# Two transformer layers: batch 1 prepared beside the first maxima, and a rearranged end of layer 0

## The chip, the cores and the metric

The kernel runs on one core of a Trainium2 chip. The metric is device time in microseconds (us). The times of the kernel before are three runs: 2031.5, 2032.39 and 2035.87, median 2032.39. Engines are PE (matrix products), DVE (vector), ACT (scalar functions), POOL (general purpose), and SP, which here only issues transfers.

## The reference

The input x is 8 batches of 1024 rows of 128 numbers. Two layers follow each other, each of an attention part and a feed-forward part, each part behind a layer normalisation and with its result added to x:

```python
x = x + _L0_attn_ref(_layernorm(x), Wq, Wkv_down, Wk_up, Wv_up, Wo)   # softmax attention, 8 heads of 32
x = x + _L0_ffn_ref(_layernorm(x), gate_w, w1, b1, w2, b2)            # 2 of 14 experts per row, gelu, 256 wide
x = x + _L1_attn_ref(_layernorm(x), Wq, Wk, Wv, Wo)                   # cumulative linear attention, 16 heads of 8
x = x + _L1_ffn_ref(_layernorm(x), router_w, W1, b1, W2, b2)          # 1 of 8 experts with a capacity, relu, 512 wide
```

In layer 0 keys and values come from a common latent of 64 numbers per row; softmax runs over all 1024 keys. The expert layer takes the softmax of 14 logits per row, the two largest, and adds the two experts' outputs weighted by their shares, plus the row it was given, cut to plus or minus 100.

## The kernel before, in words

**Attention of layer 0.** The two weights of the low-rank path are multiplied once (`combined_weights`), so that keys and values are one projection each of the normalised rows. The work is cut into 32 blocks: a group of 4 heads of one batch (`n = 2*batch + group`) by 512 queries (`qb`). A block has 16 steps, a key chunk of 128 and a pair of heads each, so there are 512 steps, in one loop whose order is written out by hand for PE, DVE and ACT (POOL runs in the order that a scheduler gives it, save for the instructions that are `pinned`).

Each step has two kinds of score products. `largest` (line 340) computes scores with queries on partitions, and DVE takes each row's maximum (line 344). `spread` and `spread_rows` turn these into three bf16 rows per head, by way of small SP transfers. `scores` (lines 379 and 380) computes them again with keys on partitions, the maximum subtracted by a product, and ACT takes the exponential (line 383). POOL adds the exponentials of two key chunks (line 208 in the profile's rows, a helper), and `weigh` (line 397) makes the numerators and, of the added pairs, the denominators. `settle` and `divide` make the quotient.

The maxima run `LEAD = 24` steps ahead of the scores. These 24 steps form the lead, a loop of its own before the main loop: it runs maxima and, after every even step from 4 on, one piece of the list `beside`: the last projection of heads group 0, the four `values` of batch 0, four projections of group 1. A piece is a product or two on PE into one of the three banks of the PSUM pool `big` and an evacuation by ACT. The maxima of the lead alternate between `big` and `sc`, the scores' pool of three.

Everything else of the attention is hung on the main loop as pieces per step, in the table `todo`. `prepare(b)` hangs batch b on the 64 steps of the batch before: statistics on DVE, the power of -0.5 on POOL, scaling on ACT, transposes on PE with a copy by ACT, four projections of group `2*b` (steps 20 to 25), four pairs of values (32 to 37), and the projections of group `2*b + 1` 64 steps later. So batch 1 is prepared in blocks 0 to 2 and, for its second group, in block 4. `complete(b)` hangs the output projection, the second normalisation and the choice of experts.

**The end of the attention.** After the last block its half batch (512 rows) goes through the same chain with nothing beside it: normalised, turned (`turned`, lines 295 to 300), logits (471), the two largest, `count`, `rank`, `places`. `count` (539 to 557) writes the marks of the two chosen experts into a table `both` whose column 0 holds the counts so far; `rank` makes each row's place within its expert. `places` (573 to 597) makes from rank and expert the index `at` and then eight moves, indirect transfers by POOL (588), each of which stores 128 rows into the table `rows_in`, sorted by expert.

**The tables of experts.** `expert_tables` (116 to 159) counts the tiles of 256 rows that each expert needs (`grid`, `tiles`, `upto`), and makes for each tile its first row in `rows_in` (`row_j`) and its expert (`exp_j`). These two are computed on one partition with shape 1 x 77 x 14, 1078 numbers per instruction.

**The tiles of layer 0.** `tiles0` runs 72 tiles. `fetch` loads a tile by SP at a row number read from `row_j` (four tiles ahead); `stage` copies the expert's weights out of the big table by DVE (886); `turn` transposes; `hidden0` multiplies and takes gelu on ACT (901, 904); `output0` multiplies again, adds bias and input rows on DVE, and stores into `rows_out` by POOL (921). PE, DVE, ACT and SP have a written order here. At tile 8 the constants of layer 1 are made. `warm` issues one unread gather by POOL. A branch (985) follows, taken only if more than 72 tiles are needed; it isn't taken with these inputs.

**Layer 1** begins with gathers from `rows_out` by POOL (1078), two per 128 rows, waits for all rows stored, and then runs its attention and its own expert tiles, for which `expert_tables` is called a second time.

Of the kernel before, what the change touches and what calls it, by code (L numbers as in the profile page):

```python
# [8 lines left out]
F32 = mybir.dt.float32  # L9
# [69 lines left out]
def tile_two_layers(  # L79
# [12 lines left out]
    for b in range(NB):  # L92
        xb = keep.tile([P, CPB, D], F32, name=f"x{b}", tag=f"x{b}")
        xs.append(xb)
    nc.sync.dma_start(out=xs[0], in_=x[0].rearrange("(c p) d -> p c d", p=P))
    cst = keep.tile([P, C_END], F32, name="cst")
# [19 lines left out]
    def expert_tables(tab, psum, ptag, counts, ne, nt):  # L116

        tot = psum.tile([P, ne], F32, name="tot", tag=ptag)  # L120
        nc.tensor.matmul(tot, lhsT=ones, rhs=counts, start=True, stop=True)
        per = CAP0 // TW0
        grid = tab.tile([P, ne, per], F32, name="grid")
        nc.vector.tensor_tensor(
            grid, tot.unsqueeze(2).to_broadcast([P, ne, per]),
            cst[:, C_TW:C_TW + per].unsqueeze(1).to_broadcast([P, ne, per]), ALU.is_gt,
        )
        tiles = tab.tile([P, ne], F32, name="tiles")
        nc.vector.tensor_reduce(tiles, grid, AX.X, ALU.add)
        upto = tab.tile([P, ne], F32, name="upto")  # L130
        nc.vector.tensor_tensor_scan(upto, ones[:, :ne], tiles, 0.0, ALU.mult, ALU.add)
        jshape = [1, nt, ne]
# [12 lines left out]
        nc.vector.tensor_tensor(hop, lead[:, 1:], lead[:, :ne], ALU.subtract)  # L145
        hops = tab.tile(jshape, F32, name="hops")
# [3 lines left out]
        nc.vector.scalar_tensor_tensor(rj, cst[0:1, C_J:C_J + nt], float(TW0), rj, ALU.mult, ALU.add)  # L150
        nc.vector.tensor_scalar(rj, rj, lead[0:1, 0:1], float(ne * REG0), ALU.add, ALU.min)
        row_j = tab.tile([1, nt], mybir.dt.int32, name="row_j")
        nc.vector.tensor_copy(row_j, rj)
        ej = tab.tile([1, nt], F32, name="ej")
        nc.vector.tensor_reduce(ej, past, AX.X, ALU.add)
        nc.vector.tensor_scalar(ej, ej, float(ne - 1), None, ALU.min)
        exp_j = tab.tile([1, nt], mybir.dt.int32, name="exp_j")
        nc.vector.tensor_copy(exp_j, ej)
        return SimpleNamespace(exp_j=exp_j, row_j=row_j, base=base, tot=tot, upto=upto)
# [30 lines left out]
    nc.gpsimd.memset(counts, 0.0)  # L190
    found = routes.tile([P, NB, 2, CPB], U32, name="found")
    layer0w = ctx.enter_context(ExitStack())
    blob = layer0w.enter_context(tc.tile_pool(name="blob", bufs=1)).tile([P, E0, B_END], F32, name="blob")

    with ExitStack() as ph:
# [30 lines left out]
        def load_rest():  # L226
            for b in range(1, NB):
                pinned(nc.sync.dma_start, out=xs[b], in_=x[b].rearrange("(c p) d -> p c d", p=P))
# [205 lines left out]
        class Finish:  # L434
# [96 lines left out]
            def weights(self):  # L531
# [4 lines left out]
                for k, p in enumerate((self.p1, self.p2)):  # L536
                    nc.vector.tensor_tensor(shares[:, k, self.b, self.c0:self.c0 + self.n], p, s, ALU.mult)

            def count(self):

                n = self.n
                both, ahead = (
                    stat0.tile([P, E0, CPB + 1], F32, name=name, bufs=1) for name in ("both", "ahead")
                )
                if n < CPB:
                    nc.vector.memset(both, 0.0)
                nc.vector.tensor_copy(both[:, :, 0], counts)
# [25 lines left out]
            def places(self):  # L573
# [13 lines left out]
                def move(j, k):  # L587
# [6 lines left out]
                    tc.add_to_no_dep_group("rows_in", ins.ins)  # L594
                    tc.keep_in_program_order(ins)

                moving.extend(lambda j=j, k=k: move(j, k) for k in range(2) for j in range(n))
# [24 lines left out]
        norms = [Norm(0, c0, CPK, xn, xT[0]) for c0 in (0, CPK)]  # L622
        combined_weights()
        for f in norms:
            f.stats(0, CPK)
            f.power()
        for f in norms:
            f.offset()
            for i in range(0, CPK, 2):
                f.scaled(i, shared=True)  # L630
            f.turned(0)
        for of_k, h in ((False, 0), (True, 0), (True, 1)):
# [38 lines left out]
        def prepare(b):  # L671

            h0, norm = 64 * (b - 1), []
            at(h0, start_norm, b, norm)
# [6 lines left out]
            h1 = h0 + (64 if b < NB - 1 else 48)  # L681
            for (of_k, i), h in zip(((True, 0), (False, 0), (True, 1), (False, 1)), (0, 1, 4, 5)):
                at(h1 + h, project, 2 * b + 1, of_k, i)

# [32 lines left out]
        for n, qb in blocks:  # L717
            for kc in range(CPB):
                for hp in range(2):
# [93 lines left out]
    counts1 = keep.tile([P, E1], F32, name="counts1")  # L813
    rows1 = dram.tile([ROWS1, RW1], F32, name="rows1")

    def load_layer1():
# [42 lines left out]
    def tiles0(ph, first, last):  # L859
# [23 lines left out]
        def stage(j):  # L883
            e = expert_of(j)
            t = work.tile([P, 1, B_END], F32, name="wt", bufs=4)
            nc.vector.tensor_copy(t, blob[:, bass.ds(e, 1), :])
            return t[:, 0, :]
# [19 lines left out]
        def output0(j, t, w, g):  # L907
            ps = py_ps.tile([P, TI0, D], F32, name="py")
            for i in range(TI0):
# [10 lines left out]
            nc.vector.tensor_tensor(y, y, t, ALU.add)  # L920
            nc.gpsimd.dma_start(  # L921
                out=rows_out[j * TW0:(j + 1) * TW0, :].rearrange("(p i) d -> p i d", i=TI0), in_=y
# [24 lines left out]
        with tc.manual_schedule(  # L947
# [9 lines left out]
            for j in range(first, last):  # L957
# [42 lines left out]
    with ExitStack() as ph:  # L1000
# [56 lines left out]
        gathered = [0]  # L1057

        def behind(ins, name, kind=mybir.DependencyClass.NoSync):
            tc.add_manual_dep(  # L1060
                ins, name, mybir.DependencyInfo(kind, mybir.DependencyReason.DATA), reason="the order of issue"
            )

# [789 lines left out]
```

## Time and profile before

The profiled execution took 2032.74 us; the span on the core is 2030.9 us; the difference lies around the program. The three timed runs have a median of 2032.39.

| | value |
|---|---|
| profiled execution, its span | 2032.74, 2030.9 us |
| granted TensorE clock, mean | 0.958 |
| busy PE, DVE, POOL, ACT | 1921.2, 1386.3, 1203.2, 1107.6 us |
| start to first maxima | 0 to 19.45 us |
| the lead (24 steps of maxima) | 19.45 to 50.89 us |
| main loop and end of attention | 50.89 to about 1305 us |
| tiles of layer 0 | 1319.99 (first transposes) to 1466.4 us |
| layer 1 | 1485.93 (first transposes) to 2030.9 us |

Busy shares are means over stages that have different limits. In the rows by slice a digit is the busy share of a fortieth of the span in tenths. A timeline line gives the start, the length, the engine, the line of the kernel, the operation, the tile written and the tiles read, and in brackets how long the engine was idle before and what ended that. SPq, POOLq and the like are an engine's own queue of semaphore, branch and transfer-issuing instructions.

### The profile page before, as it was taken

To read this page: it belongs to the slowest core of one execution; us is meant where nothing else is said; L and a number is where in the kernel's file an instruction comes from. 1 tells how busy PE (TensorE), PEld (TensorE's weight loads), DVE (VectorE), ACT (ScalarE), POOL (GpSimd) and SP (SyncE) were. 2 spreads that over 40 slices of the span, in tenths; PEclk is the share of its full clock that TensorE was granted. 3 is DMA by queue.
4 is the path that set the end of the run, shared out by engine and by line. 5 is a ranking of instruction groups with operands and counts; after the bars stand their busy time and mean duration, and the time that the engine had idled before them with its cause. 6 is when DMAs were issued, how large, how long until landed. Compare 5 with 4: busy or idle time off the path is not lost. (4 is left out here: it accounts for less than half of the span.)

```text
span 2030.9 us, 45100 instructions
## 1 busy us (share of the span) xinstructions
PE 1921.2 (95%) x17336; PEld 992.3 (49%) x17336; DVE 1386.3 (68%) x3551; ACT 1107.6 (55%) x2336; POOL 1203.2 (59%) x1316
## 2 busy tenths in 40 slices
PE   7999999999999999999999998499859999996997
PEld 3333333333333333333333333299837777775896
DVE  6667768768768768768767876656537777765453
ACT  2555565665565565655565454266536766662443
POOL 1456556667667766767766766433265566644465
PEclk9999999999999999999999998699959999996999
DMA  7000000000000000000000000044323221111331
GB/s 242 1 2 2 2 2 3 8 8 10 8 8 8 9 6 9 9 8 9 8 8 8 13 9 23 29 132 133 114 63 86 76 63 52 50 38 65 105 104 58
DMA packets 49023, 80.93 MB, mean 40 GB/s; under 512 B 13225, under 2 KB 31600, under 8 KB 48672
## 3 DMA queue, kind: packets, MB, share of 16 engines
q0 software_dynamic: 17744, 41.55, 6.2%
q1 hardware_dynamic: 27664, 28.45, 4.8%
q10 hardware_dynamic: 3392, 7.95, 1.3%
q8 instruction: 140, 2.29, 0.5%
q14 instruction: 83, 0.68, 0.1%
HBM read 42.08 MB, written 35.96 MB: 38 GB/s over the span
## 5 line engine op out<-in xcount | busy, mean ns | idle before, releaser
L344 DVE TENSOR_REDUCE nmp<-big 128x1 f32<-128x512 f32 x1000 | 641.9, 683 | 284.9 <-PE st L380 242.0
L383 ACT ACTIVATE e<-st 128x512 f32<-128x512 f32 x1000 | 544.4, 595 | 479.7 <-PE st L380 416.5
L208 POOL TENSOR_TENSOR e<-e 128x512 f32<-128x512 f32 x488 | 603.9, 1268 | 51.8 <-PE num L397 51.7
L340 PE MATMUL big<-kT,qT 32*128 32x512 f32 x2000 | 630.2, 642 | 0.1
L380 PE MATMUL st<-qT,kT 32*128 32x512 f32 x2000 | 532.9, 590 | 0.0
L397 PE MATMUL num<-e,v 128*32 128x512 f32 x3064 | 302.5, 468 | 5.9 <-ACT nums L425 5.9
L208 POOL TENSOR_TENSOR outT<-nums,dens 128x64 f32<-128x64 f32 x248 | 80.9, 327 | 353.9 <-DVE dens L415 263.0
L380 PEld LDWEIGHTS st<-qT,kT 32*128 32x128 f32 x2000 | 214.6, 192 | 3.3 <-issue 1.2
L379 PE MATMUL st<-nb,ones_h 3*128 3x512 bf16 x1000 | 212.4, 385 | 1.3 <-DVE nmp L344 1.3
L397 PEld LDWEIGHTS num<-e,v 128*32 128x32 f32 x3064 | 61.3, 108 | 294.9 <-issue 270.6
L379 PEld LDWEIGHTS <-ones_h 3*128 3x128 bf16 x1024 | 51.2, 91 | 314.9 <-issue 308.2
L340 PEld LDWEIGHTS big<-kT,qT 32*128 32x128 f32 x2000 | 194.3, 183 | 21.3 <-DVE nmp L344 16.9
L1078 POOL DMA_INDIRECT got<-rows_out,found x128 | 126.4, 987 | 94.7 <-PE tp L1113 43.3
L588 POOL DMA_INDIRECT rows_in<-xn,at x128 | 130.7, 1021 | 38.4 <-issue 29.3
L415 DVE RECIPROCAL dens<-dens 128x64 f32<-128x64 f32 x248 | 130.1, 537 | 17.5 <-ACT dens L410 17.4
L397 PE MATMUL den<-e,ones 128*32 128x512 f32 x1032 | 140.8, 615 | 0.2 <-POOL e L208 0.2
L1623 POOL DMA_INDIRECT out_x<-y,to x72 | 79.1, 1099 | 68.8 <-DVE y L1621 52.0
L1604 ACT ACTIVATE g<-ph,wt 128x256 f32<-128x256 f32 x144 | 63.8, 474 | 86.9 <-PE ph L1601 86.9
L921 POOL DMA_DIRECT2D rows_out<-y x72 | 41.8, 580 | 100.6 <-DVE y L920 93.0
L1133 ACT ACTIVATE qm<-qk,cst 128x256 f32<-128x256 f32 x128 | 54.5, 496 | 53.9 <-DVE qk L1130 53.7
L1383 POOL DMA_INDIRECT rows<-row,where x64 | 63.5, 992 | 29.2 <-issue 12.7
L911 PEld LDWEIGHTS py<-wt,g 128*128 128x128 f32 x576 | 76.0, 193 | 3.8
(286 smaller groups left out, 2921.9 us busy)
## 6 DMA issues: line engine op xcount, KB each, us to landing
xr<-rows SPq DMA_DIRECT2D x36, 257.0 KB
xr<-rows_in SPq DMA_DIRECT2D x72, 128.0 KB
rows_out<-y POOLq DMA_DIRECT2D x72, 128.0 KB, 2.3
nb<-part SPq DMA_DIRECT2D x384, 1.0 KB
blob<-in_blob ACTq DMA_DIRECT2D x8, 578.0 KB
blob<-in_blob SPq DMA_DIRECT2D x1, 4494.0 KB
x<-in_x SPq DMA_DIRECT2D x8, 512.0 KB
rows<-nil ACTq DMA_DIRECT2D x9, 257.0 KB
```

The source lines that it names most:

```text
L208: return tc.keep_in_program_order(f(*args, **kw))
L340: nc.tensor.matmul(ps, lhsT=qTs[n][r, qc * P:(qc + 1) * P], rhs=kTs[n][r, kb * BLK:(kb + 1) * BLK], start=True, stop=True,)
L344: nc.vector.tensor_reduce(nmps[n][:, h, qc, kb:kb + 1], ps, AX.X, ALU.max, negate=True)
L379: nc.tensor.matmul(st, lhsT=ones_h[r3, :], rhs=nbs[n][r3, cols], start=True, stop=False)
L380: nc.tensor.matmul(st, lhsT=kTs[n][r, kc * P:(kc + 1) * P], rhs=qTs[n][r, cols], start=False, stop=True)
L383: nc.scalar.activation(e[:, h, :], st, AF.Exp, scale=SCALE0)
L397: nc.tensor.matmul(vds[key][32 * h:32 * h + 32, cols], lhsT=ones[:, :HD0] if den else vs[b][:, kc, c0:c0 + HD0], rhs=e[:, h, cols], start= ...
L415: nc.vector.reciprocal(s[:, cols], s[:, cols])
L588: ins = nc.gpsimd.indirect_dma_start(out=rows_in, out_offset=bass.IndirectOffsetOnAxis(ap=ats[k][:, j:j + 1], axis=0), in_=xn[:, c0 + j, : ...
L911: nc.tensor.matmul(ps[:, i, :], lhsT=g[:, k, i * P:(i + 1) * P], rhs=w[:, B_W2 + k * D:B_W2 + (k + 1) * D], start=k == 0, stop=k == K0 - 1,)
L1078: ins = tc.keep_in_program_order(nc.gpsimd.indirect_dma_start(out=gots[p][:, i, k, :], out_offset=None, in_=rows_out, in_offset=bass.Indir ...
L1623: ins = nc.gpsimd.indirect_dma_start(out=out_rows, out_offset=bass.IndirectOffsetOnAxis(ap=at[:, i:i + 1], axis=0), in_=y[:, i, :], in_off ...
```

## The change

It has these parts:

- The load of x1 is issued right after that of x0, ahead of the constants.
- `combined_weights` returns its two evacuations instead of making them; each is done after the transposes of one half of batch 0.
- Batch 1's statistics and power come before the lead. Its offset, scalings, transposes, the projections of groups 1 and 2 and its values join the list `beside`, which grows from 9 to 24 pieces; the lead takes two after every odd step. `prepare(1)` keeps only the projections of group 3.
- The denominators that were made in the very last step are made two steps earlier.
- At the end, the last half batch is turned in two parts of two chunks; the table of counts is begun (`start_count`) before the logits; an unread gelu follows the last exponential.
- `expert_tables` holds tiles on partitions: `past` and `hops` have shape 128 x 14, two columns are turned by PE into rows. The function stands for both layers. In the built order the instructions of the tables stand between those of the last `places` and `softmax`: `grid` after the first ranks, the sum `tiles` before the first index.
- The first copy of expert weights waits for the last move of rows.
- The last four tiles' rows are stored by SP, and with them those of the branch not taken. `warm` is named four tiles later.

The diff, shortened:

```diff
-    nc.sync.dma_start(out=xs[0], in_=x[0].rearrange("(c p) d -> p c d", p=P))
+    for b in range(2):
+        nc.sync.dma_start(out=xs[b], in_=x[b].rearrange("(c p) d -> p c d", p=P))
...
-        past = tab.tile(jshape, F32, name="past")
-        nc.vector.tensor_tensor(
-            past, upto[0:1].unsqueeze(1).to_broadcast(jshape),
-            cst[0:1, C_J:C_J + nt].unsqueeze(2).to_broadcast(jshape), ALU.is_le,
-        )
...
-        nc.vector.tensor_tensor(hops, past, hop[0:1].unsqueeze(1).to_broadcast(jshape), ALU.mult)
-        rj = tab.tile([1, nt], F32, name="rj")
-        nc.vector.tensor_reduce(rj, hops, AX.X, ALU.add)
...
+        j = cst[:, C_TOK:C_TOK + 1]
+        past, hops = (tab.tile([P, ne], F32, name=name) for name in ("past", "hops"))
+        nc.vector.tensor_scalar(past, upto, j, None, ALU.is_le)
+        nc.vector.tensor_tensor(hops, past, hop, ALU.mult)
+        both = tab.tile([P, 2], F32, name="both")
+        nc.vector.tensor_reduce(both[:, 0:1], hops, AX.X, ALU.add)
...
+        for i in range(2):
+            nc.tensor.transpose(ps[:, i, :], both[:, i:i + 1], ident)
+        row_j, exp_j = (tab.tile([1, nt], mybir.dt.int32, name=name) for name in ("row_j", "exp_j"))
+        nc.vector.tensor_copy(row_j, ps[:, 0, :nt])
+        nc.vector.tensor_copy(exp_j, ps[:, 1, :nt])
...
-            nc.scalar.copy(wk_sb, ps[:, 0, :])
-            nc.scalar.copy(wv_sb, ps[:, 1, :])
+            return [lambda w=w, i=i: nc.scalar.copy(w, ps[:, i, :]) for i, w in enumerate((wk_sb, wv_sb))]
...
+            def start_count(self):
+                self.both = stat0.tile([P, E0, CPB + 1], F32, name="both", bufs=1)
+                if self.n < CPB:
+                    nc.vector.memset(self.both, 0.0)
+                nc.vector.tensor_copy(self.both[:, :, 0], counts)
...
+        norm = Norm(1, 0, CPB, xn, xT[1])
+        norm.stats(0, CPB)
+        norm.power()
         load_rest()
-        beside = [lambda: project(0, False, 1)]
-        beside += [lambda c2=c2: values(0, c2) for c2 in range(CPB // 2)]
-        beside += [lambda of_k=of_k, h=h: project(1, of_k, h) for h in range(2) for of_k in (True, False)]
+        beside = [norm.offset, lambda: project(0, False, 1), lambda: norm.scaled(0), lambda: norm.scaled(2)]
+        beside += [lambda c2=c2: values(0, c2) for c2 in range(2)]
+        beside += [lambda: norm.turned(0), lambda: norm.scaled(4), lambda: norm.scaled(6)]
+        beside += [lambda c2=c2: values(0, c2) for c2 in range(2, 4)]
+        beside += [lambda: norm.turned(CPK)]
+        beside += [
+            lambda n=n, of_k=of_k, h=h: project(n, of_k, h) for n in (1, 2) for h in range(2) for of_k in (True, False)
+        ]
+        beside += [lambda c2=c2: values(1, c2) for c2 in range(CPB // 2)]
...
-            if j >= 4 and j % 2 == 0 and beside:
-                beside.pop(0)()
+            if j % 2:
+                for _ in range(2):
+                    if beside:
+                        beside.pop(0)()
...
-                    elif summing is not None:
+                    elif summing is not None and h < STEPS - 1:
...
+                    if h == STEPS - 3:
+                        weigh(*summing, den=True)
...
-        norm.turned(0)
+        f.start_count()
+        for i in range(0, CPK, 2):
+            norm.turned(i, 2)
         for piece in f.choice():
             piece()
+            if piece == f.exponential2:
+                nc.scalar.activation(stat0.tile([P, 1], F32, name="unread0"), ones[:, :1], AF.Gelu)
...
+            ins = nc.vector.tensor_copy(t, blob[:, bass.ds(e, 1), :]).ins
+            if j == 0:
+                behind(ins, last_move[0], mybir.DependencyClass.Sync)
...
-            nc.gpsimd.dma_start(
+            engine = nc.gpsimd if j < NT0_MAIN - 4 else nc.sync
+            engine.dma_start(
...
-                if j == NT0_MAIN - 8:
+                if j == NT0_MAIN - 4:
                     warm()
```

More of the change, by code (lines that the diff above doesn't have):

```diff
@@ L131, in expert_tables @@
         nc.vector.tensor_tensor_scan(upto, ones[:, :ne], tiles, 0.0, ALU.mult, ALU.add)
-        jshape = [1, nt, ne]
-        past = tab.tile(jshape, F32, name="past")
-        nc.vector.tensor_tensor(
-            past, upto[0:1].unsqueeze(1).to_broadcast(jshape),
-            cst[0:1, C_J:C_J + nt].unsqueeze(2).to_broadcast(jshape), ALU.is_le,
-        )
         base = tab.tile([P, ne], F32, name="base")
@@ L145, in expert_tables @@
         nc.vector.tensor_tensor(hop, lead[:, 1:], lead[:, :ne], ALU.subtract)
-        hops = tab.tile(jshape, F32, name="hops")
-        nc.vector.tensor_tensor(hops, past, hop[0:1].unsqueeze(1).to_broadcast(jshape), ALU.mult)
-        rj = tab.tile([1, nt], F32, name="rj")
-        nc.vector.tensor_reduce(rj, hops, AX.X, ALU.add)
[L150 to L158, printed above, removed]
+        j = cst[:, C_TOK:C_TOK + 1]
[4 more added lines that the diff above has]
+        nc.vector.tensor_reduce(both[:, 0:1], hops, AX.X, ALU.add)
+        nc.vector.scalar_tensor_tensor(both[:, 0:1], j, float(TW0), both[:, 0:1], ALU.mult, ALU.add)
+        nc.vector.tensor_scalar(both[:, 0:1], both[:, 0:1], lead[:, 0:1], float(ne * REG0), ALU.add, ALU.min)
+        nc.vector.tensor_reduce(both[:, 1:2], past, AX.X, ALU.add)
+        nc.vector.tensor_scalar(both[:, 1:2], both[:, 1:2], float(ne - 1), None, ALU.min)
+        ps = psum.tile([1, 2, P], F32, name="both_t", tag=ptag)
+        for i in range(2):
[3 more added lines that the diff above has]
+        nc.vector.tensor_copy(exp_j, ps[:, 1, :nt])
         return SimpleNamespace(exp_j=exp_j, row_j=row_j, base=base, tot=tot, upto=upto)
@@ L191, in tile_two_layers @@
     found = routes.tile([P, NB, 2, CPB], U32, name="found")
+    last_move = []
     layer0w = ctx.enter_context(ExitStack())
@@ L226, in load_rest @@
         def load_rest():
-            for b in range(1, NB):
+            for b in range(2, NB):
                 pinned(nc.sync.dma_start, out=xs[b], in_=x[b].rearrange("(c p) d -> p c d", p=P))
@@ L537, in weights @@
                     nc.vector.tensor_tensor(shares[:, k, self.b, self.c0:self.c0 + self.n], p, s, ALU.mult)
+            both = None
+            def start_count(self):
[3 more added lines that the diff above has]
+                nc.vector.tensor_copy(self.both[:, :, 0], counts)
             def count(self):
                 n = self.n
[L542 to L547, printed above, removed]
+                ahead = stat0.tile([P, E0, CPB + 1], F32, name="ahead", bufs=1)
+                if self.both is None:
+                    self.start_count()
+                both = self.both
                 nc.vector.tensor_tensor(
@@ L595, in move @@
                     tc.keep_in_program_order(ins)
+                    last_move[:] = [ins.ins.name]
                 moving.extend(lambda j=j, k=k: move(j, k) for k in range(2) for j in range(n))
@@ L622, in tile_two_layers @@
         norms = [Norm(0, c0, CPK, xn, xT[0]) for c0 in (0, CPK)]
-        combined_weights()
+        weights_ready = combined_weights()
         for f in norms:
@@ L631, in tile_two_layers @@
             f.turned(0)
+            weights_ready.pop(0)()
         for of_k, h in ((False, 0), (True, 0), (True, 1)):
             project(0, of_k, h)
-        load_rest()
-        beside = [lambda: project(0, False, 1)]
-        beside += [lambda c2=c2: values(0, c2) for c2 in range(CPB // 2)]
-        beside += [lambda of_k=of_k, h=h: project(1, of_k, h) for h in range(2) for of_k in (True, False)]
+        xn = work.tile([P, CPB, D], F32, name="xn", bufs=1)
+        xT[1] = work.tile([P, T], F32, name="xT")
+        norm = Norm(1, 0, CPB, xn, xT[1])
+        norm.stats(0, CPB)
+        norm.power()
+        load_rest()
+        beside = [norm.offset, lambda: project(0, False, 1), lambda: norm.scaled(0), lambda: norm.scaled(2)]
[7 more added lines that the diff above has]
+        beside += [lambda c2=c2: values(1, c2) for c2 in range(CPB // 2)]
         for j in range(LEAD):
@@ L673, in prepare, with prepare_first @@
             h0, norm = 64 * (b - 1), []
+            if b > 1:
+                prepare_first(b, h0, norm)
+            h1 = h0 + (64 if b < NB - 1 else 48)
+            for (of_k, i), h in zip(((True, 0), (False, 0), (True, 1), (False, 1)), (0, 1, 4, 5)):
+                at(h1 + h, project, 2 * b + 1, of_k, i)
+        def prepare_first(b, h0, norm):
             at(h0, start_norm, b, norm)
@@ L679, in prepare @@
                 at(h0 + h, values, b, i)
-            h1 = h0 + (64 if b < NB - 1 else 48)
-            for (of_k, i), h in zip(((True, 0), (False, 0), (True, 1), (False, 1)), (0, 1, 4, 5)):
-                at(h1 + h, project, 2 * b + 1, of_k, i)
         def complete(b):
@@ L814, in tile_two_layers, with behind @@
     rows1 = dram.tile([ROWS1, RW1], F32, name="rows1")
+    def behind(ins, name, kind=mybir.DependencyClass.NoSync):
+        tc.add_manual_dep(
+            ins, name, mybir.DependencyInfo(kind, mybir.DependencyReason.DATA), reason="the order of issue"
+        )
     def load_layer1():
@@ L885, in stage @@
             t = work.tile([P, 1, B_END], F32, name="wt", bufs=4)
-            nc.vector.tensor_copy(t, blob[:, bass.ds(e, 1), :])
+            ins = nc.vector.tensor_copy(t, blob[:, bass.ds(e, 1), :]).ins
+            if j == 0:
+                behind(ins, last_move[0], mybir.DependencyClass.Sync)
             return t[:, 0, :]
@@ L1057, in tile_two_layers @@
         gathered = [0]
[L1059 to L1062, printed above, removed]
         products = []
```

## The prediction

> **What bounds the kernel now.** The page's engine table, read first, gives PE 95% of a span of 2030.9 us, DVE, the next, 68%. So work taken off PE is time, and other work is time only where PE stands still. The rows by slice (51 us each, digits are tenths) show where that is:
>
> ```profile
> PE   7999999999999999999999998499859999996997
> PEclk9999999999999999999999998699959999996999
> ```
>
> PE pauses at the start, in slice 25 (end of the attention) and in slice 28 (layer 0 to layer 1): the change's three places. Second, the table of busy time by stretch: window, length, then busy us and count of PE, PEld, DVE, ACT, POOL, then the clock, DMA share, GB/s. The first row is the lead (24 steps of maxima), the next four are score blocks 0 to 3, the last two the boundaries:
>
> ```profile
> 19.40:50.80 31.40, 30.17 (x124) 11.86 (x123) 28.69 (x51) 5.86 (x10) 0.00 (x0) 1.00 0.57 221
> 50.80:88.90 38.10, 38.01 (x283) 14.45 (x287) 27.14 (x58) 21.05 (x41) 19.75 (x16) 0.91 0.01 1
> 88.90:126.60 37.70, 37.61 (x305) 12.04 (x307) 25.14 (x45) 21.36 (x39) 18.85 (x23) 1.00 0.01 2
> 126.60:164.40 37.80, 37.80 (x309) 13.46 (x309) 25.64 (x45) 20.81 (x39) 22.12 (x26) 1.00 0.01 1
> 164.40:198.80 34.40, 34.40 (x293) 11.47 (x289) 25.65 (x45) 18.44 (x35) 22.11 (x25) 1.00 0.01 2
> 1303.90:1320.00 16.10, 0.31 (x3) 0.21 (x2) 11.64 (x37) 0.00 (x0) 10.45 (x15) 0.50 0.14 47
> 1466.50:1485.90 19.40, 0.00 (x0) 0.00 (x0) 2.77 (x11) 1.31 (x4) 9.46 (x11) 0.57 0.15 41
> ```
>
> Block 3 has no preparation in it: 34.4 us is a bare block. Blocks 1 and 2 carry batch 1's preparation on a full PE. In the lead DVE is busy 28.69 of 31.40 us, yet PE is occupied too. The timeline of the lead (start, length, engine, line, operation; a row per matmul or run of them) tells how:
>
> ```profile
> 33.47 0.69 PE L340 MATMUL big<-kT,qT 32*128 32x512 f32 x1
> ...
> 34.80 1.13 PE L315 MATMUL val<-wv_sb,xT 128*128 128x256 f32 x4
> 35.86 0.69 PE L340 MATMUL big<-kT,qT 32*128 32x512 f32 x1
> ...
> 37.63 1.13 PE L329 MATMUL prj<-xT,wk_sb 128*128 128x512 f32 x2
> ...
> 50.89 0.37 PE L379 MATMUL st<-nb,ones_h 3*128 3x512 bf16 x1 [1.32 <-DVE nmp L344]
> ```
>
> Two steps of maxima take PE 1.33 us (33.47 to 34.80) where banks are free, 1.77 (35.86 to 37.63) where they aren't; a piece between them takes 1.06 (34.80 to 35.86). The four reduces of a pair cost DVE 4 x 0.60 = 2.4 us. Bare, the lead is DVE's; with a piece per pair a cycle is 2.39 to 2.83 (33.47 to 35.86, 34.80 to 37.63), near 2.6; with two pieces it becomes PE's. The timeline of both boundaries:
>
> ```profile
> 1304.69 0.17 DVE L584 TENSOR_SCALAR at<-to 128x4 uint32<-128x4 f32 x1
> 1305.62 0.96 POOL L588 DMA_INDIRECT rows_in<-xn,at  x1 [9.48 <-issue]
> 1319.99 1.42 PE L892 MATMUL px<-cst,xr 128*128 128x128 f32 x4 [15.79 <-DMA xr<-rows_in]
> 1321.84 1.28 ACT L904 ACT_TABLE_LOAD   x1
> 1466.74 0.54 POOL L921 DMA_DIRECT2D rows_out<-y  x1 [0.35 <-DVEq L986]
> 1474.59 1.00 POOL L1078 DMA_INDIRECT got<-rows_out,found  x1 [7.31 <-issue]
> 1485.93 0.86 PE L1113 MATMUL tp<-cst,xn 128*128 128x128 f32 x2 [20.41 <-DMA got<-rows_out,found]
> ```
>
> PE stands 15.8 us from the first move's index to the first fetched tile, and 20.4 us at the layer boundary, whose gather starts 7.85 us after the last store was issued.
>
> **Start: -0.8.** Two weight copies leave the front of ACT's queue, ahead of the first normalised rows: two of about 0.37 (an ACT copy of 128x256 from PSUM, by the timeline's xt<-px row). Batch 1's 16 statistics (about 2.6 us of DVE) fall into DVE's idle 10.75 to 20.61, before the first maxima; x1's load was issued right behind x0's already, so nothing waits. Its power goes ahead of the zero fills on POOL, first read by the first moves hundreds of us later: 0. Eight scalings are ACT's, busy 5.86 of 31.4: 0, and at 0.37 each about 3 us if ACT had no room.
>
> **Lead: +6.0.** 24 pieces instead of 9; 19 have PE work (9 projections, 8 values, 2 of four transposes). In the changed kernel's built order 8 pairs of steps get two PE pieces, 3 one, 1 none. A double cycle is 1.33 to 1.77 plus 1.06 plus 0.86 (a second piece back to back): 3.25 to 3.7; I take 3.35, since DVE's slack (2.4 of it) frees banks early. 8 x 3.35 + 3 x 2.6 + 2.4 + 0.3 for the end = 37.3 against 31.4. Bounds +5.2 and +10.
>
> **Blocks 0 to 2: -8.3.** They lose what the lead gained. Block 1 (four transposes, four projections) and block 2 (values) come down to the bare 34.4: -3.3 and -3.35, by the table above. Block 0 loses four transposes (0.9); of the 1.5 us by which it is otherwise over a bare block I drop half, because the clock (0.91) was at half for 52.8 to 59.6, and a lead that ends later may meet that differently. -7.5 to -9.0. Early net: -2.3 for these two parts, -3.1 with the start. The gain is that work beside DVE's reduces costs less than alone: 15 extra pieces fit partly into PE's idle slots and serial pairs.
>
> **Attention's end and the move to the tiles: -0.9.** The last denominators but one go before the last scores, not after: those start 0.66 later, the last den ends 0.25 later (+0.25). Transposes evacuated in two parts let the first logits run beside the second copy: -0.63 (half the 1.12 + 0.59 of tp and its copy, less an extra copy). The counts' memset and copy leave the path: -0.23. But the 128x448 comparison (0.61) and its reduce (0.62) now stand on DVE between ranks and the first index; some falls in a latency gap of 0.31 there: +0.8. So the first move starts at about 1305.8: net +0.2. Behind DVE's inserted reduce are the second index and all 8 moves; POOL has nothing else. The moves, spaced 1.27, were stretched to 1.22 and 1.36 where 0.96 is usual, beside the two 1x1078 products on DVE; those shrink to 128x14: -0.66. The first fetch waited for its row number (cast at 1316.35, loaded by 1317.50) and left at 1317.92, 0.56 after the last row had landed at 1317.36; the number will be ready sooner: -0.3 to -0.56, say -0.43. Sum -0.9, bounds 0 and -1.8.
>
> The weight copies (0.5 each, four) now wait for the last row's landing, and so go beside POOL's memsets (0.96 the longest); behind the waiting copy on DVE stand the other three and the first output's sum, and the first hidden product waits for it. Row: the last move took 0.96 with a copy beside it, not lengthened. [...] The first hidden layer needs only copy one, some 3.5 us behind the landing (0.3 issue, 2.07 fetch, 1.2 turning and copying): by row 0[...]. I take 0.
>
> The table load of gelu moves from 1321.84 into idle ACT time. [...] The row has 1.28, and PE is busy without a pause from 1319.99 to 1326 under it (next tile's transposes and hidden products): 0. I take the row.
>
> **Layer boundary: -4.8.** The last four row stores go from POOL to SP. In the list for the branch line POOL has an INC_SWDGE_SEM, which the new order no longer contains:
>
> ```profile
> L986 POOLq INC_SWDGE_SEM  x1: 2462/2462/2462, 1467.8 to 1467.8; - x1
> ```
>
> It begins at 1467.8 and reports at 1470.2; POOL's waits go on to 1471.3, then 3.3 us without any record until the gather. At the kernel's end the same instruction (1.37 us at 2023.8) is followed by a POOL drain of 4.89 us, where other drains take at most 0.11, so I hold the silent 3.3 us for its aftermath. Without it: SP issues at 1466.5, lands about 2.03 later (an xr fetch's time on that queue; the POOL store took 2.02), up to 0.7 of extra semaphore sums on SP beside it, 0.3 to the gather: 1469.8 for 1474.59. Bounds -1.4 (silent gap stays) and -5.2. SP has no fetch left behind these stores.
>
> **Zero:** the probe `warm` is named later in the source, but its place in POOL's order is the same; layer 1's tables end (1872.2) before the last scatter lands (1875.8), with 3.6 us of cover.
>
> **Sum:** -0.8 + 6.0 - 8.3 - 0.9 - 4.8 = -8.8, from the profiled 2032.74 to 2023.9. The median is 2032.39, 0.35 lower: **2023.6**.
>
> **Rivals.** *The lead only moves work* (15%): an extra piece costs there what it saves later; early part 0, 2026.7. For: PE is already busy 30.17 of 31.40 there. Against: 1.33 against 1.77 per pair shows slack. *The silent gap isn't the INC's* (12%): the boundary gives 1.4, 2027.0; both together (4%), 2030.1. *Slower* (5%): pieces and maxima share three PSUM banks, and the row at 50.89 waits 1.32 for one. If each of two pieces holds its bank through its ACT copy (0.59) and the pair waits again, a double cycle is 1.77 + 1.32 + 2 x (1.06 + 0.59) = 6.4 us, 8 x 3.05 = +24: 2048. It decides from a cycle of 4.45 us, where 8 x 1.1 eats all the gain; against it, single cycles of 2.6 already include such waits. *Better* (9%): the lead shifts the half-clock stretch away (up to 1.7 per 3.4 us of it) or the tail gives its bound: 2019. The forecast's own case has 55%.
>
> **How the numbers follow.** The forecast case with its bounds reaches 2020 to 2027.3; with the better case and the two middle rivals the range is 2018.5 to 2029. A measurement can tell about 0.2% (4.1 us): faster is below 2028.3. The forecast, the better case and most of the two rivals lie there: 0.87; same 0.08; slower 0.05.
>
> **What would show it.** First score at 56 to 57 instead of 50.9; blocks 1 and 2 near 34.4; the first fetch about 1.2 us nearer to the last index; the first gather 3 to 4 us behind the last add instead of 8.1, and no INC_SWDGE_SEM there. Wrong it is if double cycles exceed 4 us, if blocks 0 to 2 don't shrink, or if POOL stays silent after the stores.

## The result and the profile after

The changed kernel took 2021.81 us (median of five runs, 2016.75 to 2022.93), the kernel before 2032.39 (five runs). The ratio is 0.9939, 95% interval [0.9921, 0.9956]: faster by 0.4 to 0.8%. The forecast was 2023.6 with a range of 2018.5 to 2029. The profiled execution took 2022.9 us with a span of 2021.0, against 2032.74 and 2030.9. Four of the variants below (the late branch, two stores by SP, no wait of the copy, no unread gelu) ran at a time when the kernel before itself took 2067.63 us, with a longer layer 1, so only their stages up to layer 1 are used.

The two traces, cut at the same instructions, give the stages in us. "Forecast" is the working of the prediction for that stage. Blocks count from the first exponential, 1.3 us after the lead ends in both.

| stage | before | after | difference | forecast |
|---|---|---|---|---|
| start to first maxima | 19.45 | 19.16 | -0.29 | -0.8 |
| lead | 31.44 | 35.87 | +4.43 | +6.0 |
| blocks 0 / 1 / 2 | 36.78 / 37.69 / 37.75 | 33.35 / 34.32 / 34.38 | -10.17 | -8.3 |
| block 3 to last exponential | 1118.67 | 1119.49 | +0.82 | with the next row |
| last exponential to transposes of the last half batch | 12.65 | 12.01 | -0.64 | together +0.25 |
| those transposes to the first tile's | 24.30 | 23.13 | -1.17 | -1.15 |
| tiles of layer 0 | 146.45 | 146.77 | +0.32 | 0 |
| last sum of a tile to first gather | 8.15 | 2.73 | -5.42 | -4.8 |
| first gather to first product of layer 1 | 11.35 | 11.35 | 0 | 0 |
| layer 1 up to the first scatter of results | 404.39 | 406.52 | +2.13 | 0 |
| from there to the end | 140.62 | 140.67 | +0.05 | 0 |

The table of busy time by stretch, of the kernel after (window, length, busy us and count of PE, PEld, DVE, ACT, POOL, then clock, DMA share, GB/s), has the lead, blocks 0 to 2 and the two boundaries:

```profile
19.20:55.00 35.80, 34.58 (x156) 14.46 (x155) 30.08 (x54) 14.23 (x27) 0.00 (x0) 1.00 0.51 207
56.30:89.60 33.30, 33.30 (x269) 11.59 (x270) 21.68 (x37) 17.45 (x32) 18.08 (x15) 1.00 0.01 1
89.70:124.00 34.30, 34.30 (x293) 11.47 (x289) 25.64 (x45) 18.41 (x35) 18.82 (x23) 1.00 0.01 2
124.00:158.40 34.40, 34.40 (x293) 11.47 (x289) 25.64 (x46) 18.45 (x35) 22.11 (x25) 1.00 0.01 1
1298.80:1313.00 14.20, 0.59 (x2) 0.09 (x2) 4.90 (x31) 0.00 (x0) 9.37 (x13) 0.50 0.17 52
1459.80:1473.80 14.00, 0.00 (x0) 0.00 (x0) 2.77 (x11) 1.29 (x4) 8.90 (x10) 0.61 0.20 56
```

Blocks 1 and 2 are bare blocks now. DVE is busy 30.1 us of a lead of 35.8, PE 34.6: the lead has become PE's, as foreseen. At the end of attention DVE has 4.90 us of work where it had 11.64, and the layer boundary is 14.0 us long, not 19.4. The timeline of the lead after shows two cycles with two pieces each:

```profile
38.54 0.69 PE L340 MATMUL big<-kT,qT 32*128 32x512 f32 x1
...
39.61 1.13 PE L329 MATMUL prj<-xT,wk_sb 128*128 128x512 f32 x2
40.57 1.02 PE L329 MATMUL prj<-xT,wq_sb 128*128 128x512 f32 x2
41.64 0.69 PE L340 MATMUL big<-kT,qT 32*128 32x512 f32 x1
...
43.54 1.13 PE L329 MATMUL prj<-xT,wk_sb 128*128 128x512 f32 x2 [0.56 <-DVE nmp L344]
...
45.83 0.69 PE L340 MATMUL big<-kT,qT 32*128 32x512 f32 x1
```

The first, from 38.54 to 41.64, takes 3.10 us: the pair of steps 1.07, the pieces 0.96 and 1.07. All banks were free when the pair began, since DVE had caught up during the two pieces (it then stood idle for 0.61 us, until 39.69, waiting for the pair's products); so the pair cost less than the 1.33 of before. Six of the eight double cycles take these 3.10 us. The second one here, from 41.64 to 45.83, takes 4.19, with the transpose of `spread_rows` in it and a wait of 0.56 us for DVE behind that. The first of the lead, from 22.27 to 27.12, takes 4.85, because the pair ahead of it has no piece and left DVE behind; together those two take 5.84.

The timeline of the attention's end, after:

```profile
1297.59 0.61 DVE L125 TENSOR_TENSOR grid<-tot,cst 128x448 f32<-128x448 f32 x1
...
1298.24 0.62 DVE L130 TENSOR_REDUCE tiles<-grid 128x14 f32<-128x448 f32 x1
1298.77 0.16 DVE L590 TENSOR_SCALAR at<-to 128x4 uint32<-128x4 f32 x1
...
1299.70 0.96 POOL L594 DMA_INDIRECT rows_in<-xn,at  x1 [9.37 <-issue]
...
1310.80 2.21 DVE L924 COPY wt<-blob 128x642 f32 x4 [8.71 <-DMA rows_in<-xn,at]
1311.31 0.85 POOL L864 MEMSET nil<- 128x514 f32 x1 [1.80 <-DVE wt L924]
1313.00 0.47 PE L933 MATMUL px<-cst,xr 128*128 128x128 f32 x1 [11.32 <-DMA xr<-rows_in]
```

The first index waits behind the two inserted instructions, as worked out. The four weight copies, about 0.5 us each, take 2.21 us together beside POOL's memsets, and the first memset takes 0.85 where it took 0.53: they do hold each other up. (Without the copies beside it, in the variant below whose first copy doesn't wait, that memset takes 0.53 again.)

The layer boundary, after:

```profile
1462.51 1.00 POOL L1116 DMA_INDIRECT got<-rows_out,found  x1 [8.49 <-DVE row L1129]
...
1473.86 0.47 PE L1151 MATMUL tp<-cst,xn 128*128 128x128 f32 x1 [15.01 <-DMA got<-rows_out,found]
```

The last tile's sum ended at 1459.78, so the gather follows 2.73 us behind it, and layer 1 begins on PE 11.35 us behind the gather, as before. The 2.73 us are not a constant of this kernel: in its second profile, taken later, they are 3.88.

### The profile page after: what moved, and what is told of

Read it like the earlier page. It is cut to its first block, busy times and chain, and to the rows that moved or that the text cites. A ratio compares the mean times of both kernels' runs of the same rounds, so it can differ in the third digit from the quotient of the medians.

```text
span 2021.0 us, 45115 instructions
## 1 busy us (share of the span) xinstructions
PE 1918.9 (95%) x17340; PEld 991.8 (49%) x17340; DVE 1379.7 (68%) x3551; ACT 1108.8 (55%) x2338; POOL 1201.7 (59%) x1312
```

## The experiments

Stage lengths come from one profile of each kernel. Where the clock is the same, the lead, the blocks and the steps from the last transposes to the first tile repeat within about 0.1 us from kernel to kernel, so they separate causes that the timed runs cannot: in the later comparisons the kernel before itself ranged from 2021.6 to 2039.8 us. The first gather of layer 1 doesn't repeat so well once the last four tiles are stored by SP: over eight such profiles it comes 2.72 to 3.88 us behind the last sum. It follows the landing of the last store by 0.82 to 1.01 us in all eight, and that landing is what varies, from 1.72 to 3.06 us behind the last sum; why isn't shown. With all stores by POOL, as before, it comes at 8.14 or 8.15 in three profiles.

**The lead alone.** The kernel before with the loads of x1, the deferred weight copies and the new list of pieces, and nothing else of the change.

```diff
-        beside = [lambda: project(0, False, 1)]
+        beside = [norm.offset, lambda: project(0, False, 1), lambda: norm.scaled(0), lambda: norm.scaled(2)]
...
-            if j >= 4 and j % 2 == 0 and beside:
-                beside.pop(0)()
+            if j % 2:
+                for _ in range(2):
+                    if beside:
+                        beside.pop(0)()
```

> The kernel before with only the lead's part (loads, weight copies, batch 1 prepared beside the first maxima). Theory: the early gain of 6.0 us comes whole with it: first score at 55.0 (50.9 before), block 3 begins at 158.4 (164.4 before), no half clock between 52 and 60; time about 2026.4. Rival: 2.5 of the 6.0 are only a half-clock stretch that the changed kernel happened to miss; then a stretch of it shows up again near block 0 and block 3 begins at 160.9, time about 2029. Rival of the prediction (work only moved): 164, 2032.

Measured: lead 35.87, blocks 33.35, 34.31 and 34.38 us, the same as with the whole change; boundary stages as before (24.28 and 8.14); 2023.46 us, ratio 0.9956 [0.9936, 0.9976]. The early gain comes whole with the lead.

**The stores alone.** The kernel before with its last four row stores, and the branch's, on SP.

```diff
-            nc.gpsimd.dma_start(
+            engine = nc.gpsimd if j < NT0_MAIN - 4 else nc.sync
+            engine.dma_start(
```

> The kernel before with only its last four row stores, and those of the branch, issued by SP. Theory: the first gather of layer 1 comes 2.7 us after the last sum of a tile, as in the changed kernel, and not 8.1 as before; time about 2032.4 - 5.4 = 2027. Rival (the boundary's gain needs the other parts too): 8.1 stays, 2032.

Measured: 2.72 us from the last sum to the gather; 2024.0 us, ratio 0.9974 [0.9957, 0.9992]. The boundary's gain needs no other part of the change. This profile gave something more: its lead is the old one, but block 0 took 34.37 us, not 36.78.

**The kernel before once more, and the changed kernel once more.**

> The kernel before once more, to see whether the half-clock stretch of 52.8 to 59.6 us belongs to it. If it does, block 0 lasts 36.8 us again; if it is the clock's free play, 34.4 us, as in the variant that differs from it only in the last stores.

> The changed kernel once more. If missing the half clock in blocks 0 to 2 belongs to the change, block 0 lasts 33.35 us again, as in eight profiles with this lead so far, and block 3 begins 139.2 us after the first maxima; if not, up to 3.4 us later. Time 2017 to 2023.

Measured: block 0 of the kernel before took 40.92 us; that of the changed kernel 33.35. The stretches of the variant with the stores alone (lead, block 0):

```profile
18.70:51.20 32.50, 31.23 (x124) 11.99 (x123) 28.83 (x51) 5.86 (x10) 0.00 (x0) 0.95 0.58 224
52.50:86.90 34.40, 34.40 (x277) 12.51 (x277) 25.69 (x56) 20.96 (x42) 19.77 (x16) 1.00 0.01 2
```

and block 0 of the kernel before in its second profile:

```profile
52.80:93.70 40.90, 40.90 (x277) 14.61 (x276) 25.83 (x57) 21.14 (x42) 19.91 (x16) 0.79 0.01 1
```

The work is equal (277 products in both); what differs is the clock, 1.00 against 0.79. In the three profiles with the old lead a half-clock stretch of 3.4, 6.8 or 17.1 us began once at 23.8, 52.8 or 53.8 us. In the eleven with the new lead none began before 1206 us. So the old block 0 without it is 34.37 us, the clock cost 2.4 us of it in the first profile and 6.6 in the second, and the change removes it in every profile seen. Why it does isn't shown. One difference is on record: with the old lead PE pauses for 1.3 us just ahead of the first score, in all three profiles, and in two of them the stretch begins 1.9 and 2.3 us behind that pause; in the third it came before, and none followed the pause. With the new lead PE has no pause over 0.6 us from the first maxima to the end of block 0. No run takes the pause alone away. In the profile with the stretch of 17.1 us, block 0 had its mean clock of 0.79 while PE was busy for 40.90 of 40.90 us.

The changed kernel's second run of comparisons gave 2014.19 us, ratio 0.9932 [0.9908, 0.9956]. In its second profile the first gather came 3.88 us behind the last sum, so the boundary gained 4.3 us there and not 5.4. Its layer 1 was 11.5 us shorter than in the first profile, at the same work. The stretch up to the first scatter, first profile and second:

```profile
1474.00:1880.00 406.00, 380.46 (x5380) 275.07 (x5381) 271.42 (x1059) 242.49 (x624) 227.38 (x247) 0.88 0.21 64
```

```profile
1472.00:1867.00 395.00, 366.74 (x5382) 266.45 (x5383) 271.22 (x1060) 242.64 (x625) 227.78 (x248) 0.92 0.22 65
```

The clock is 0.88 in one and 0.92 in the other, and DVE, ACT and POOL have equal work: the difference is the clock's. That is as much as the whole gain, so a difference of one or two microseconds can't be read from these totals.

**Who holds up POOL at the layer boundary.** The changed kernel with all 72 tiles stored by POOL, and only the branch's stores on SP, so that INC_SWDGE_SEM is absent:

```diff
-            engine = nc.gpsimd if j < NT0_MAIN - 4 else nc.sync
+            engine = nc.gpsimd if j < NT0_MAIN else nc.sync
```

> The changed kernel, but the last four row stores of the 72 tiles go by POOL again; only the stores in the branch that isn't taken stay with SP. Theory: POOL's INC_SWDGE_SEM at the branch, which is there only because the branch holds POOL transfers, made the gap; without it the first gather comes 3 to 3.6 us after the last sum and the time stays within 1 us of 2021.8. Rival: a store in POOL's own queue is what delays POOL's next gather; then the gather comes 7.5 to 8.1 us after the last sum, and the time is about 2027.

Measured: 6.63 us, between the two; 2016.97 us, ratio 0.9932 [0.9909, 0.9955]. The INC, with the two waits that go with it, accounts for 1.5 of the 5.4 us. POOL's last semaphore wait ends at 1461.42, and the gather starts 3.30 us after that, just as in the kernel before (in the changed kernel 0.7 us lie between the two): the silent stretch is not the INC's. The theory put on record with the prediction falls. The timeline of POOL in this variant:

```profile
1458.39 0.54 POOL L964 DMA_DIRECT2D rows_out<-y  x1 [0.35 <-DVEq L1029]
1464.72 0.99 POOL L1116 DMA_INDIRECT got<-rows_out,found  x1 [5.79 <-issue]
```

Next, POOL reaching the branch late without storing:

```diff
+            if j == NT0_MAIN - 1:
+                nc.gpsimd.tensor_tensor(late_sum, y[:, 0, 0:1], y[:, 0, 0:1], ALU.add)
```

> The changed kernel with one addition: POOL, which no longer stores the last four tiles, adds one column of the last tile's sum into a tile that nobody reads, so that it reaches the branch as late as in the kernel before, but with no store behind it and no INC_SWDGE_SEM at the branch. Theory now (after the variant with POOL stores and no INC still had its first gather 6.63 us after the last sum): POOL's silent 3.3 us belong to what comes after a branch passed late, the gather starting no sooner than some 5.6 us after it; then the gather comes about 6 us after the last sum. Rival: it is the store just issued by POOL that holds up its gather; then 2.7 us, as in the changed kernel.

Measured: 3.26 us, with the branch passed at 1467.23 and the gather at 1469.80. Passing the branch late doesn't hold POOL up. Then only two tiles, and only one, stored by SP:

```diff
-            engine = nc.gpsimd if j < NT0_MAIN - 4 else nc.sync
+            engine = nc.gpsimd if j < NT0_MAIN - 2 else nc.sync
```

> The changed kernel, but only the last two tiles' rows are stored by SP, not the last four, so POOL's last store and its branch come some 2.9 us before the last sum. If the gather can start no sooner than 6.3 us after POOL's last store (5.6 after its branch), it comes about 3.6 us after the last sum. If it only matters that the very last store isn't POOL's, 2.7.

> The changed kernel, but only the very last tile's rows are stored by SP; POOL stores the three before it, so its last store comes some 0.6 to 0.9 us before the last sum. Two rules fit the runs so far (first gather 6.63 us after the last sum with all stores on POOL, 3.0 with two on SP). If POOL's gather is held up for a time after POOL's last store (5.4 us or more but not much over 6.3, counted from the store's start), it comes 4.7 to 5.7 us after the last sum. If only a wait for POOL's own last store makes POOL late, it comes 2.7 to 3.3 us after it.

Measured: 3.01 and 3.52 us to the first gather, so neither rule held: the first gather is early. But another gather is late. POOL's timeline with one tile stored by SP (last sum at 1455.99):

```profile
1455.39 0.54 POOL L964 DMA_DIRECT2D rows_out<-y  x1 [1.21 <-DVE y L961]
1459.51 1.00 POOL L1116 DMA_INDIRECT got<-rows_out,found  x1 [3.57 <-DVE row L1129]
1462.54 0.98 POOL L1116 DMA_INDIRECT got<-rows_out,found  x1 [2.04 <-issue]
1463.83 0.95 POOL L1116 DMA_INDIRECT got<-rows_out,found  x1 [0.31 <-issue]
```

and with two (last sum at 1461.78):

```profile
1464.78 1.00 POOL L1116 DMA_INDIRECT got<-rows_out,found  x1 [4.82 <-DVE row L1129]
1466.08 0.98 POOL L1116 DMA_INDIRECT got<-rows_out,found  x1 [0.30 <-issue]
1468.27 0.95 POOL L1116 DMA_INDIRECT got<-rows_out,found  x1 [1.20 <-issue]
```

The stop has moved, to the second gather with one store gone from POOL and to the third with two, and it ends at 6.55 and 6.49 us behind the last sum, with none gone (the first gather) at 6.63. The gathers behind a stop come later, and layer 1 starts on PE 13.22 and 12.25 us behind the first gather instead of 11.35.

Whether the held gather sits at the same count each time can be read from the traces. Among all of POOL's transfers the held one is the 205th in every kernel that shows the stop: the kernel before, and the variants with none, one and two stores gone. It isn't the same instruction by count: among all of POOL's records the three variants' held gathers are the 1300th, 1299th and 1298th, since most stores take a semaphore wait along when they go. With four stores gone the 205th transfer is the fifth gather, due 7.8 us behind the last sum, when the stop is over. So either a set number of POOL's transfers or something timed, until some 6.5 us behind the last sum, is involved; a variant with the four stores on SP and four transfers added to POOL elsewhere would tell more, and wasn't tried. Loading a new stretch of instructions is the obvious rival, a guess of the author's; but the traces record the packets of the two instruction queues, and none falls in any of these stops. In the one of the kernel before, 1471.30 to 1474.59, no packet of any queue moves. The cause stays open.

**The tables behind the last index.** Order of issue alone: `grid` waits for the second `at`.

```diff
+            tc.add_manual_dep(
+                ins, last_at[0], mybir.DependencyInfo(
+                    mybir.DependencyClass.NoSync, mybir.DependencyReason.DATA), reason="the order of issue"
+            )
```

> The changed kernel, but the experts' tables start on DVE only behind the last index (order of issue alone). Theory: the first index comes 0.76 us sooner, the tables are still done long before the last row lands, so the first move, the last move and the first transposes of a tile all come 0.76 us sooner, counted from the transposes of the last half batch: 22.4 instead of 23.13 us to the first tile's. Rival: the comparison and its sum on DVE now lie beside POOL's moves and stretch two of them by 0.3 to 0.4 each, as two were stretched before; then 0 to 0.3 is left. Both are too small for the timed runs: about 2021.1.

Measured: from the ranks' reduce to the first index 0.55 us, not 1.31; moves 9.79, not stretched; from the half batch's transposes to the first tile's 22.45 instead of 23.13. The 0.68 us are there, in the one profile of this variant: the early comparison was a cost of the change with no return. 2014.86 us, ratio 0.9917 [0.9891, 0.9944].

**No wait of the first weight copy.**

```diff
-            if j == 0:
-                behind(ins, last_move[0], mybir.DependencyClass.Sync)
```

> The changed kernel, but the first copy of expert weights doesn't wait for the last move, so the four copies run beside the moves. By the row of the kernel before (a last move of 0.96 us beside a copy) the eight moves keep their 9.8 us from first start to last end and the first tile's transposes stay 23.1 us behind those of the last half batch. [...] POOL's memsets fall back from 0.85 to 0.53 (the first).

Measured: the moves take 10.22 us, the first tile's transposes come 23.65 us behind the half batch's, 0.5 later. All four copies ran during a single move:

```profile
1306.47 0.96 POOL L594 DMA_INDIRECT rows_in<-xn,at  x1 [0.30 <-issue]
1307.73 1.38 POOL L594 DMA_INDIRECT rows_in<-xn,at  x1 [0.30 <-issue]
```

That move took 1.38 where its neighbours take 0.96. So four copies on DVE did hold up a move on POOL beside them, by 0.42 us: more than the row of before said, where a move beside one copy took 0.96.

**No unread gelu.** Its instruction left out.

> The changed kernel without the unread gelu, so that the table is loaded at the first tile's gelu again. By the row (PE busy without a pause under the load) the first output product stays 5.3 us behind the first transposes and nothing changes after it[...].

Measured: the load is back at the first tile (1.28 us at 1321.50) and the first output product follows the transposes by 5.21 us, 5.30 in the changed kernel. Nothing is lost: the row was right, and the load's 1.28 us do not reach the path. The same distance plays from 4.30 to 5.30 over the kernels with the unread gelu, so one profile alone would say little; but in the variant with the stores alone, which also loads at the first tile, it is 4.19.

**The best parts together.** The tables behind the index, and the last denominators in the last step again.

```diff
-                    elif summing is not None and h < STEPS - 1:
+                    elif summing is not None:
...
-                    if h == STEPS - 3:
-                        weigh(*summing, den=True)
```

> The changed kernel with the tables behind the last index and with the last denominators made in the last step again, as before. Theory: from the last exponential to the transposes of the last half batch 12.64 us instead of 12.01, but the last exponential comes 0.86 sooner, so 0.23 gained; tables as measured, 0.68 gained; together 0.9 us under the changed kernel, which the timed runs can't resolve: about 2021.

Measured: 22.38 us between the two sets of transposes and 12.64 from the last exponential; 2016.82 us, ratio 0.9937 [0.9914, 0.9959]. No version here is told apart from the changed kernel by the timed runs; by its stages this one is some 0.7 us shorter for the tables. The denominators' part shows in the last five exponentials, which take 2.21 us from start to start here and in the lead alone, 3.07 in the changed kernel: moved denominators delay the last exponential by 0.86, and the transposes follow it 0.63 sooner (12.01 against 12.64), +0.23 in sum.

## Why the prediction was right, point by point

**Start.** The first maxima came at 18.6 to 20.0 us in the three profiles with the old start and at 17.7 to 19.2 in the eleven with the new one. The two overlap, so the 0.8 us forecast is neither shown nor excluded.

**Lead and blocks.** The mechanism held: fifteen more pieces beside DVE's reduces cost less there than alone. Two terms were mis-sized. A double cycle was put at 3.35 us and took 3.10 six times out of eight, because two pieces give DVE time to free every bank and the pair falls to 1.07 (the 1.33 that were read as "where banks are free" still held waiting). The other two took 4.19 and 4.85, over the 4 us that were named as a sign of being wrong. All eight with the pair that has no piece took 28.6 us for the 29.2 reckoned, the three with one piece 7.3 for 7.8, and the 0.3 at the end weren't needed; so the lead grew by 4.4, not 6.0. The clock's part of block 0 was put at -0.75 and was -2.4 in this pair of profiles. Without any half-clock stretch the lead and blocks 0 to 2 gain 4.43 - 1.02 - 3.37 - 3.37 = -3.3 us, where the forecast's terms without its clock share give -1.55. With it they gain 5.7, against -2.3 forecast.

**End of attention.** Every term came out within a tenth or so: transposes in two parts -0.64 (forecast -0.63), counts -0.22 (-0.23), comparison and sum ahead of the index +0.76 to the move's start (+0.8), moves -0.66 (-0.66), fetch -0.40 (-0.43), denominators +0.23 (+0.25).

**Weight copies and table load.** Both were taken at nothing. For the load this was right. The copies' wait, whose worth was also set at 0, is worth 0.5 us, and the copies beside the memsets cost no time that reaches PE: the first hidden product waited for the second tile's transposes.

**Layer boundary.** -5.4 in the first profile and -4.3 in the second, against -4.8: right in size, wrong in cause. (The forecast's own terms, 1466.5 + 2.03 + 0.7 + 0.3, add up to 1469.5 and not 1469.8, so to -5.1; and the landing put at 2.03 us behind its issue came 1.7 to 3.0 behind it.) The step that failed is "I hold the silent 3.3 us for its aftermath". Without the INC 6.63 of 8.15 us stayed, close to the rival that the silent gap isn't the INC's (-1.4; it measured -1.5). The changed kernel gains as much all the same, which for that step is luck: with four stores gone from POOL no gather meets the stop, and what makes the stop stays open above.

**The sum.** Some 0.6 us more at the boundary and 2.9 more early (start and clock included) were partly taken back by layer 1 (+2.1, at a clock of 0.88 against 0.89) and the tiles (+0.3, at 0.98 in both). So -9.9 stands for -8.8, with errors of opposite sign; the clock's share in that is chance. With the half clock of block 0 and the play of the tiles and of layer 1 left out, the stages give -0.3 - 3.3 + 0.2 - 1.2 - 5.4 = -10.0 us with the first profile's boundary and -8.9 with the second's, where the forecast without its clock share is -8.05.

**Rivals.** The lead doesn't only move work. One of its eight double cycles passed the 4.45 us from which the slower case would have decided, and only with what the pair ahead of it had left over; six took 3.10.

## What to carry to other kernels

Work put beside another engine's bottleneck is to be priced by the whole cycle: a second piece cost 1.07 us of PE, but it also let DVE free the banks, and in six cycles of eight the next pair took 1.07 where 1.33 had been reckoned. Where totals carry a clock that plays by several microseconds (11.5 here, in layer 1), cut the traces at the same instructions and compare stages. When an engine goes silent without a record, test its suspected cause by taking that alone away: here the instruction next to the gap had made only 1.5 of 5.4 us.

## What the runs showed of the hardware

- The clock fell to half for 17.1 us within a block in which PE was busy without a pause (40.90 of 40.90 us, with a mean clock of 0.79). Between two profiles of the changed kernel layer 1 alone differed by 11.5 us with it.
- POOL stood still without a record for 3.3 us ahead of its first gather behind the layer boundary, ending 6.63 us after the last sum (8.15 with an INC_SWDGE_SEM ahead of it). As one and two stores left POOL the stop moved to the second and third gather, there 2.0 and 1.2 us long and ending at 6.55 and 6.49; each time it was POOL's 205th transfer, and no packet of instructions moved in it.
- The last store on SP landed 1.7 to 3.0 us behind its issue over eight profiles, and the gather that waits for it moved along.
- Four weight copies on DVE lengthened one indirect transfer of POOL from 0.96 to 1.38 us, and beside memsets four copies took 2.21 us together.
- Semaphore waits on POOL took 0.087 us each when nothing was left to wait for: in the variant with all tiles stored by POOL ten of them run one behind the other from 1460.60 to 1461.42.
